# Half of the fourth batch's query projection moved from slot 1 to slot 0, a fifth gap in slot 0, and the first gate weights requested at the opening of slot 1

## The chip, the cores and the metric

The kernel runs on one core of a Trainium2 chip. The time is the device time of one execution in microseconds (us); the kernel before has a median of 847.64 us over 3 runs (847.49 to 848.31). The core has five engines: TensorE (PE, matmuls; its weight loads are shown as PEld), VectorE (DVE), ScalarE (ACT), GpSimd (POOL) and SyncE (SP, which here issues nearly all DMA transfers from one queue in order). Each engine works through its own list of instructions in order and waits on semaphores for the others.

## What is computed

One transformer block in float32 on `x` of 4 batches x 512 tokens x 512 features: attention after a layer norm, added to `x`, and then a gated feed-forward network after another layer norm, added again.

```python
def _layernorm(x, axis=-1, eps=1e-05):
    m = jnp.mean(x, axis=axis, keepdims=True)
    v = jnp.var(x, axis=axis, keepdims=True)
    return (x - m) / jnp.sqrt(v + eps)

# attention: 32 query heads, 8 key/value heads, 16 features per head
q = (resid @ Wq).reshape(B, T, N_HEADS, D_HEAD).transpose(0, 2, 1, 3)
k = (resid @ Wk).reshape(B, T, N_KV_HEADS, D_HEAD).transpose(0, 2, 1, 3)
v = (resid @ Wv).reshape(B, T, N_KV_HEADS, D_HEAD).transpose(0, 2, 1, 3)
q = q * cos + _rotate_half(q) * sin
k = k * cos + _rotate_half(k) * sin
att = einsum('bhgqd,bhkd->bhgqk', qg, k) / math.sqrt(D_HEAD)
att = jnp.where(causal, att, -jnp.inf)
ctx = einsum('bhgqk,bhkd->bhgqd', softmax(att), v)
out = ctx.reshape(B, T, D_MODEL) @ Wo

# feed-forward, hidden width 1376
y = (silu(xt @ W_gate.T) * (xt @ W_up.T)) @ W_down.T

x = x + attention(_layernorm(x))
x = x + feed_forward(_layernorm(x))
```

## The kernel before

Batches are counted from 0, so "the fourth batch" is batch 3. The program is one long list of instructions whose order is written out by hand. Its backbone is the attention of 32 **groups**; a group is one batch, one of four blocks of heads and one half (`GROUPS`), and there are eight to a batch. While a group's exponentials, masks and averages (`averages`, L1113, the matmuls named `av`) are made, the scores of the group two further on are taken for their bounds: each group has four **visits** (`visits`), in each of which `both_scores` (L1022, matmuls named `sc`) fills two pairs of PSUM banks, ScalarE takes exponentials of one (`exponentials`, tile `e`), and VectorE finds each row's bound in the other (`greatest`, L1035, tile `low`). A **last visit** (`last_visit`, L1056) follows and then the averages. The masks of `e` are made on POOL (`causal`, L1096). `masked` (L972) prepares a group's queries `qa` on POOL, and `turned_round` and `laid_out` carry the bounds to them through DRAM, one group ahead of their use.

**Slots.** `slot(b, steps)` (L1239) runs the eight groups of batch `b` and lays a list of **dense steps**, which belong to other work, into the gaps between the visits. Each step is a pair of a nominal cost in us and a closure. `gap(n)` adds `shares[n] / 8` of the list's total cost to the allowance, and `fill` (L1206) takes steps while the cost done, plus half the next step's, is within it. Slot 0 uses its first shares tuple and four gaps a group; slots 1 to 3 use the second tuple and a fifth gap, after the averages.

**Projections.** `projections(b, n)` (L375) gives, for a batch, `begin`, four steps `turned` and 48 steps `rest`: 8 for the keys, 8 for the first block of queries, 8 for the values and 8 for each of three further blocks of queries. A step of 0.43 nominal us (0.45 for values) is an eighth of a 512-column product; steps 0 to 3 of a key or query block use tokens 0 to 255, steps 4 to 7 tokens 256 to 511. A finished block of keys or queries is **rotated** (`rotated`, L347): two halves on VectorE (0.73 and 0.69) with a product or sum each on POOL. In slot 0 (`copied`) ScalarE first copies the bank to SBUF. Keys are also **spread** (`spread` in `keys`, L419): one shuffle on VectorE and four operations on POOL, at L425. The weights `wq`, `wk` and `wv` lie in the tile `shared` (`flat`), of which the gate and up weights later take three places in turn: place 2 is that of `wk` and `wv`, places 0 and 1 that of `wq`.

**Normalised rows.** For batches 2 and 3, `begin` puts twelve steps into the queue `calm`: statistics (kinds "a" and "b") and the normalisation (kind "c", L401) of each of four tiles of 128 tokens, on ScalarE, with three small POOL operations for each "b". One calm step is taken at each call of `odd_steps` (L259), except in visit 3, where `holding` is set. For batch 3 each "c" then puts a **flip** into the queue `aside`: `flipped` (L311) transposes the tile on VectorE in blocks (L314), writes it to DRAM with four DMAs (L318, `flip<-u`), and loads the tile before it back turned (L320, `xnT<-flip`, 256 KB); with the last tile both remaining loads go out. "Flip 1" and "load 1" are those of tile 1, and so on, from 0 to 3. `tail(i)` in `turned` takes from `calm` or `aside` until tile `i` is flipped, before the keys' first step.

**Helper queues.** `odd_steps(us, banks)` is called in every visit after `greatest` with a budget of us for VectorE: in slot 0 1.3, 0.95, 0.95 and 1.05 in visits 0 to 3, and 1.4 after the averages. With `banks` at 2 (visit 0) it takes waiting rotation halves (`full`) ahead of the queue `aside`, with 1 behind it, with 0 none. `holding` keeps POOL's work in visit 3 back until `last_visit` has issued `masked`.

**The seam.** `early` is the list of slot 0: what is left of batch 1's projections, batch 2's whole projections, and batch 3's keys, first query block and values. The copies of gate and up weights within DRAM (`copies`) are threaded into its first 40 steps. The list of slot 1 starts with `start1`: the twelve steps of batch 3's second query block and half its third, the output projection of batch 0 (`attended`, L492; its `outp` takes four products, one for each of `cx[0]` to `cx[3]`, per tile of 128 tokens, in two portions of 1.72), `load_f(0)`, the remaining twelve steps of queries with the tail of the second layer norm, and `load_f(1)`. `load_f` (L538) requests the gate and up weights of one block of 128 hidden features. Then follows the feed-forward network of batch 0 (`ordinary`, `edge`, `down`).

Of the kernel before, what the change touches and what calls it, by code (L numbers as in the profile page):

```python
# [74 lines left out]
def preln_block_kernel(  # L75
# [99 lines left out]
    def load_w(t, src):  # L175
        nc.sync.dma_start(out=t, in_=src.rearrange("(k p) m -> p k m", p=P))
# [3 lines left out]
    thin = [True]  # L180
# [4 lines left out]
    def emptied(n):  # L185
        for _ in range(n):
            for _, step in full.popleft():
                step()
# [70 lines left out]
    def odd_steps(us, banks=1):  # L259

        if calm and not holding[0]:
            calm.popleft()()
        for n in range(len(soon)):
            left, step = soon.popleft()
            if left > 0:
                soon.append((left - 1, step))
            else:
                aside.appendleft(step)
        while True:
            bank = full and full[0]  # L270
            queue = (unread and later) or (banks == 2 and bank) or aside or (banks and bank) or later
            if not queue:
                return
            us -= queue[0][0]
            if us < -0.15:
                return
            do(queue)
            if full and not full[0]:
                full.popleft()
# [4 lines left out]
    def pool_steps(n):  # L284
        for _ in range(min(n, len(idle))):
            idle.popleft()[1]()
# [251 lines left out]
    def load_f(f):  # L538
        if f < whole:
            wgu[f] = shared[:, (f + 2) % 3, :, :, :]  # L540
            for a, w in enumerate((wg, wu)):
                load_w(wgu[f][:, a, :, :], w[:, ts(f, P)])
# [76 lines left out]
    def after(step):  # L619
        return 0.0, step  # L620
# [401 lines left out]
    def both_scores(h, g, visit):  # L1022


        for c, i, j, heads in visit:
            for late in (False, True):
                for r in heads:
                    if h < len(GROUPS):
                        plain_half(h, r, i, plain[:, r % 2, c : c + P * (i + 1)], 0 if late else 64)
                    else:  # L1030
                        less_half(g, r, j, plain[:, r % 2, c : c + T - P * j], 64 if late else 0)
                for r in (2, 3) if heads[0] == 0 else (0, 1):
                    less_half(g, r, j, less[:, r % 2, c : c + T - P * j], 64 if late else 0)
# [16 lines left out]
    def all_greatest(h, visit):  # L1050
        if h < len(GROUPS):
            for c, i, j, heads in visit:
                for r in heads:
                    greatest(h, r, i, plain[:, r % 2, c : c + P * (i + 1)])

    def last_visit(h, g):  # L1056

        for r in range(4):
            less_score(g, r, 2, pairs[r // 2][:, r % 2, : 2 * P])
        if h < len(GROUPS):  # L1060
            for half in (64, 0):
                for r in range(4):
                    plain_half(h, r, 1, pairs[r // 2][:, r % 2, 2 * P :], half)
        for n in (0, 1):
            heads = slice(2 * n, 2 * n + 2)
            exponentials(e2[:, heads, :], pairs[n][:, :, : 2 * P])
            causal(e2, 0, heads)
        holding[0] = False
        masked(g + 3)
        release()  # L1070
        if h < len(GROUPS):
            for r in range(4):
                greatest(h, r, 1, pairs[r // 2][:, r % 2, 2 * P :])

    def turned_round(g):
        if g >= len(GROUPS):
            return
        t = small.tile([P, 32], F32, tag="turned", name="turned", bufs=2)
        nc.vector.transpose(t, low[g % 3])
        nc.sync.dma_start(out=lowest[g % 2], in_=t)  # L1080

    def laid_out(g):

        if g >= len(GROUPS):
            return
        rows = qa[g].rearrange("(r s) (i a q) -> r s i a q", r=4, i=NT, a=4)[:, 16 * (1 - GROUPS[g][2])]
        src = lowest[g % 2].rearrange("(a u r i) q -> u i r a q", a=4, u=2, r=4)[0]
        for a in (0, 2):
            nc.sync.dma_start(out=rows[:, 0, a : a + 2], in_=src[0][:, 2 - a : 4 - a])
        for i in range(1, NT):  # L1090
            nc.sync.dma_start(out=rows[:, i], in_=src[i])

    def exponentials(dst, src):
        nc.scalar.activation(dst, src, AF.Exp, scale=1.0 / math.sqrt(DH))  # L1094

    def causal(e, c, heads=slice(0, 4), exchanged=False):  # L1096

        for rows, base in ((slice(0, 64), -64), (slice(64, P), 0)) if exchanged else ((slice(0, P), 0),):
            nc.gpsimd.affine_select(  # L1099
                out=e[rows, heads, c : c + P],  # L1100
                in_=e[rows, heads, c : c + P],
                compare_op=ALU.is_ge,
                fill=0.0,
                base=base,
                pattern=[[0, heads.stop - heads.start], [1, P]],
                channel_multiplier=-1,
            )
# [65 lines left out]
    begin3, turned3, rest3, _ = projections(3, 3)  # L1173
    begin2, turned2, rest2, load2 = projections(2, 2)
    begin1, turned1, rest1, _ = projections(1, 1, then=load2)
# [30 lines left out]
    def fill(steps, upto, done):  # L1206
        while steps and done + steps[0][0] / 2 <= upto:
            cost, step = steps.popleft()
            step()
            done += cost  # L1210
            if not thin[0]:
                do(aside)
        return done
# [25 lines left out]
    def slot(b, steps):  # L1239

        steps = deque(steps)
        total = sum(cost for cost, _ in steps)
        done, part = 0.0, 0.0
        groups = range(8 * b, 8 * b + 8)
        thin[0] = copied[0] = b == 0
        narrow[0] = True

        shares = (0.2, 0.225, 0.2875, 0.2875, 0.0) if thin[0] else (0.19, 0.19, 0.22, 0.22, 0.18)

        def upcoming(n):  # L1250

            upto, us = part + total * shares[n] / 8, 0.0
            for cost, _ in steps:
                if done + us + cost / 2 > upto:
                    break
                us += cost
            return us

        def gap(n):
            nonlocal done, part  # L1260
            part += total * shares[n] / 8
            pool_steps((3, 2, 2, 0, 3)[n])
            done = fill(steps, part, done)

        for g in groups:
            h = g + 2
            laid_out(g + 1)
            for n, visit in enumerate(visits):
                e = (e0, e0, e1, e1)[n]
                if h < len(GROUPS):  # L1270
                    both_scores(h, g, visit)
                    exponentials(e[:, slice(0, 2) if n % 2 else slice(2, 4), :], less)
                elif n % 2 == 0:
                    both_scores(h, g, visit)
                    exponentials(e[:, 2:4, :], less)
                    exponentials(e[:, 0:2, :], plain)
                if n == 1:
                    causal(e0, 0)
                if n == 3:
                    causal(e1, 0)  # L1280
                    causal(e1, 3 * P, exchanged=True)
                all_greatest(h, visit)
                holding[0] = n == 3
                if thin[0]:
                    odd_steps((1.3, 0.95, 0.95, 1.05)[n], (2, 1, 1, 0)[n])
                else:
                    odd_steps(min(0.8 * upcoming(n) - (0.4, 0.4, 0.8, 0.8)[n], 2.3))
                gap(n)
            last_visit(h, g)
            turned_round(h)  # L1290
            averages(g)
            odd_steps(1.4)
            if not thin[0]:
                gap(4)
        thin[0] = copied[0] = narrow[0] = False
        emptied(len(full))
        if b == B - 1:
            do(later, len(later))
        for cost, step in steps:
            step()  # L1300
# [10 lines left out]
        nc.scalar.dma_start(out=homes[1], in_=spill)  # L1311

    turns = [step for pair in zip(turned2, *[iter(rest1[-8:])] * 2) for step in pair]
    early = [*rest1[16:-8], *turns, begin3, *rest2, *turned3, *rest3[:-24]]
    for u in range(whole):
        early.insert(4 * u + 4, after(lambda u=u: copies(u)))
    slot(0, early)
# [1 line left out]
    before, behind = attended(0, by_pe=(2, 3))  # L1319
# [18 lines left out]
    for u in range(whole):  # L1338
# [3 lines left out]
        asides += [(at + 1.0 * n, lambda n=n, combine=combine: combine(n)) for n in range(4)]  # L1342
    asides += [(6.0, spilled), (34.0, load_down), (34.1, load_rest)]
    start1 = [
        before[0],
        *rest3[-24:-12],
        *before[1:],
        after(lambda: load_f(0)),
        *rest3[-12:-1],
        *behind,  # L1350
        rest3[-1],
# [16 lines left out]
    before, behind = attended(1)  # L1368
# [15 lines left out]
    before, behind = attended(2)  # L1384
# [3 lines left out]
    before, behind = attended(3)  # L1388
# [36 lines left out]
```

## Time and profile before

| | |
|---|---|
| Median of 3 runs | 847.64 us (847.49 to 848.31) |
| The profiled execution | 848.06 us, of which the span 845.8 us |
| TensorE busy | 822.5 us, 97% of the span |
| VectorE, POOL, ScalarE busy | 545.5, 352.5 and 231.3 us |
| DMA traffic | 101.57 MB, mean 120 GB/s |
| Slot 0 (its first scores to those of slot 1) | 49.8 to 173.6 us |
| Granted TensorE clock | 1.00 |

A profile line of the timeline reads: start and length in us, engine, source line, operation, what it writes and reads, shape, and count; in brackets the engine's idle time just before, and what ended it. On TensorE matmuls are pipelined, and their modelled ends overlap the next start by some 0.07 us. A line of busy time by stretch reads: the stretch, its length, then busy us (and instructions) of PE, PEld, DVE, ACT and POOL, the granted clock, the DMA share and GB/s. The names in the profile are those of tiles, and several things share one tile: `wd_sb` also holds batch 3's projections and batch 1's turned rows; `xnT` stands for two tiles, one of which is batch 3's.

### The profile page before, as it was taken

To read this page: it belongs to the slowest core of one execution; us is meant where nothing else is said; L and a number is where in the kernel's file an instruction comes from. 1 tells how busy PE (TensorE), PEld (TensorE's weight loads), DVE (VectorE), ACT (ScalarE), POOL (GpSimd) and SP (SyncE) were. 2 spreads that over 40 slices of the span, in tenths; PEclk is the share of its full clock that TensorE was granted. 3 is DMA by queue.
4 is the path that set the end of the run, shared out by engine and by line. 5 is a ranking of instruction groups with operands and counts; after the bars stand their busy time and mean duration, and the time that the engine had idled before them with its cause. 6 is when DMAs were issued, how large, how long until landed. Compare 5 with 4: busy or idle time off the path is not lost.

```text
span 845.8 us, 28256 instructions
## 1 busy us (share of the span) xinstructions
PE 822.5 (97%) x11980; PEld 452.2 (53%) x11980; DVE 545.5 (65%) x1601; ACT 231.3 (27%) x342; POOL 352.5 (42%) x514
## 2 busy tenths in 40 slices
PE   6999999999999999999999999999999999999998
PEld 5654444544333335333555555436655556788887
DVE  7877777778555554458677776686877633656632
ACT  1045654422232322222233232222323331011100
POOL 4575574773544344223265634532244444101130
PEclk9999999999999999999999999999999999999999
DMA  8533304003764742253344632325333534545811
GB/s 259 124 96 78 91 16 91 5 3 64 232 191 144 235 137 77 88 200 77 84 155 140 196 115 66 115 47 151 96 97 103 162 106 148 119 146 174 291 33 50
DMA packets 149517, 101.57 MB, mean 120 GB/s; under 512 B 59696, under 2 KB 137264, under 8 KB 149136
## 3 DMA queue, kind: packets, MB, share of 16 engines
q1 hardware_dynamic: 149104, 94.01, 38.3%
q10 hardware_dynamic: 288, 5.77, 1.8%
q8 instruction: 94, 1.54, 0.8%
q14 instruction: 31, 0.25, 0.1%
HBM read 78.32 MB, written 25.17 MB: 122 GB/s over the span
## 4 chain that ended last, share of the span: by engine, by line
PE 76%; DVE 12%; POOL 4%; DMA 3%; issue 2%; ACT 1%; SPq 1%; POOLq 0%; DVEq 0%; ACTq 0%
PE mm L299 38%; PE mm L296 14%; PE sc L993 12%; DVE junk L1039 6%; PE av L1121 6%; PE sc L1006 4%; PE mm L590 2%; POOL e L1099 1%; DMA shared<-packed 1%; PE mm L582 1%; DVE st L218 1%; DVE rot L358 1%; ACT e L1094 1%; POOL home L425 1%; POOL qa L978 1%
## 5 line engine op out<-in xcount | busy, mean ns | idle before, releaser
L1039 DVE CUSTOM_DVE_ANT_0 junk<-sc,mask 128x128 f32<-128x128 f32 (+3 forms) x512 | 251.2, 491 | 139.0 <-PE sc L1006 78.4
L1094 ACT ACTIVATE e<-sc 128x1024 f32<-128x1024 f32 (+1 forms) x192 | 165.5, 882 | 384.4 <-PE sc L1006 300.7
L299 PE MATMUL mm<-xnT,shared 128*32 128x256 f32 (+1 forms) x3520 | 244.2, 420 | 2.3 <-DMA shared<-in_wg 1.5
L1099 POOL TENSOR_SCALAR_AFFINE_SELECT e<-e 128x512 f32<-128x512 f32 (+2 forms) x192 | 105.7, 560 | 225.4 <-ACT e L1094 222.3
L299 PEld LDWEIGHTS mm<-xnT,shared 128*32 128x32 f32 x3520 | 116.9, 110 | 113.0 <-issue 62.8
L993 PE MATMUL sc<-home,qa 32*64 32x512 f32 (+6 forms) x2048 | 156.1, 421 | 6.5 <-DVE low L1039 3.0
L1006 PE MATMUL sc<-qa,home 32*64 32x512 f32 (+6 forms) x2048 | 152.2, 427 | 1.5 <-DVE low L1039 0.8
L993 PEld LDWEIGHTS sc<-home,qa 32*64 32x64 f32 x2048 | 66.8, 131 | 90.2 <-DVE low L1039 29.1
L1121 PE MATMUL av<-e,home 128*32 128x512 f32 (+3 forms) x1024 | 81.9, 438 | 1.8 <-POOL e L1099 1.6
L296 PE MATMUL mm<-xnT,shared 128*128 128x256 f32 x360 | 80.3, 383 | 1.0 <-DMA shared<-packed 1.0
L296 PEld LDWEIGHTS mm<-xnT,shared 128*128 128x128 f32 x360 | 68.3, 192 | 12.8 <-issue 2.2
L299 PE MATMUL mm<-wd_sb,home 128*32 128x256 f32 (+3 forms) x848 | 71.4, 470 | 0.0
L1006 PEld LDWEIGHTS sc<-qa,home 32*64 32x64 f32 x2048 | 58.8, 130 | 22.5 <-issue 8.7
L1121 PEld LDWEIGHTS av<-e,home 128*32 128x32 f32 x1024 | 30.5, 109 | 47.2 <-issue 35.0
L299 PEld LDWEIGHTS mm<-wd_sb,home 128*32 128x32 f32 (+1 forms) x848 | 28.2, 110 | 36.9 <-issue 28.2
L299 PE MATMUL mm<-wo_sb,cx 128*32 128x512 f32 x384 | 45.4, 595 | 0.0
L797 POOL TENSOR_TENSOR wd_sb<-home 128x256 f32<-128x256 f32 x15 | 11.4, 759 | 75.6 <-DVE home L721 75.3
L1039 DVE DVE_READ_ACCUMULATOR2_ANT low<- 128x1 f32 x512 | 42.4, 83 | 0.0
L221 POOL TENSOR_TENSOR rstd<-rstd,neghalf 128x1 f32<-128x1 f32 x24 | 16.0, 667 | 56.8 <-DVE rstd L220 56.7
L1145 POOL TENSOR_TENSOR inv<-us,inverse 128x256 f32<-128x256 f32 x32 | 20.9, 654 | 44.5 <-DVE inverse L1138 44.3
L359 POOL TENSOR_TENSOR rot<-rot,rope_sb 128x512 f32<-128x512 f32 x18 | 25.7, 1425 | 23.0 <-DVE rot L358 22.8
L721 POOL TENSOR_TENSOR home<-home,u 128x512 f32<-128x512 f32 x20 | 25.2, 1281 | 21.2 <-DVE u L757 21.2
(146 smaller groups left out, 855.6 us busy)
## 6 DMA issues: line engine op xcount, KB each, us to landing
shared<-packed SPq DMA_DIRECT2D x90, 256.0 KB
flip<-u SPq DMA_DIRECT2D x88, 64.0 KB
packed<-xnT SPq DMA_DIRECT2D x10, 512.0 KB
xnT<-flip SPq DMA_DIRECT2D x18, 256.0 KB
wd_sb<-differences SPq DMA_DIRECT2D x7, 640.0 KB
shared<-packed SPq DMA_DIRECT2D x30, 128.0 KB
rows<-in_x SPq DMA_DIRECT2D x14, 256.0 KB
out<-rows SPq DMA_DIRECT2D x13, 256.0 KB
```

The costliest lines, as they stand in the source:

```text
L296: nc.tensor.matmul(out, lhsT=lhsT, rhs=rhs, start=start, stop=stop)
L299: nc.tensor.matmul(out[c : c + 32], lhsT=lhsT[:, c : c + 32], rhs=rhs, start=start, stop=stop)
L359: put(lambda: engine.tensor_tensor(rot, rot, sin, ALU.mult))
L590: nc.tensor.matmul(ps[96:P, ts(q, P)], lhsT=rest_w[:, a, kq, 32 * q : 32 * q + 32], rhs=xnTs[0][:, kq, most:], start=kq == 0, stop=kq == N ...
L721: engine.tensor_tensor(g, g, t, ALU.mult)
L993: nc.tensor.matmul(dst[at : at + 64, :n], lhsT=qa[g][rows_of(r), q : q + 64], rhs=keys_of(g)[rows_of(r), :n], start=True, stop=True,)
L1006: nc.tensor.matmul(dst[at : at + 64, first_q:], lhsT=keys_of(g)[rows_of(r), k : k + 64], rhs=qa[g][rows_of(r), P * j + first_q :], start=True,
L1039: nc.vector.tensor_tensor_reduce(out=junk[:, :n], in0=src, in1=mask[:, T - n : T] if i else mask[:, T:], scale=-1.0, scalar=BIG, op0=ALU.a ...
L1094: nc.scalar.activation(dst, src, AF.Exp, scale=1.0 / math.sqrt(DH))
L1099: nc.gpsimd.affine_select(out=e[rows, heads, c : c + P], in_=e[rows, heads, c : c + P], compare_op=ALU.is_ge, fill=0.0, base=base, pattern ...
L1121: nc.tensor.matmul(av[32 * r : 32 * r + 32, P * j :], lhsT=v[:, j, 4 * (m // 2) + r, DH * (1 - hf) : DH * (3 - hf)], rhs=e[:, r, c : c + n ...
L1145: nc.gpsimd.tensor_tensor(us[m][:, :, hf, :], turned[0][:, :, hf, :], by, ALU.mult)
```

## The change

Twelve of the 24 query steps of batch 3 that slot 1 ran first are put at the end of slot 0's list (one whole block of queries and half the next). Slot 0's nominal total goes from 47.00 to 52.16 us and slot 1's from 117.82 to 112.66. Slot 0 gets the fifth gap that the other slots have, with a share of 0.07, and the other four shares are scaled. `load_f(0)` is put ahead of batch 0's output projection as the first step of slot 1.

```diff
-        shares = (0.2, 0.225, 0.2875, 0.2875, 0.0) if thin[0] else (0.19, 0.19, 0.22, 0.22, 0.18)
+        shares = (0.19, 0.21, 0.265, 0.265, 0.07) if thin[0] else (0.19, 0.19, 0.22, 0.22, 0.18)
...
             averages(g)
             odd_steps(1.4)
-            if not thin[0]:
-                gap(4)
+            gap(4)
...
-    early = [*rest1[16:-8], *turns, begin3, *rest2, *turned3, *rest3[:-24]]
+    early = [*rest1[16:-8], *turns, begin3, *rest2, *turned3, *rest3[:-12]]
...
     start1 = [
-        before[0],
-        *rest3[-24:-12],
-        *before[1:],
         after(lambda: load_f(0)),
+        *before,
         *rest3[-12:-1],
```

`before[0]` is the opening of `attended(0)`, which does nothing for batch 0.

## The prediction

> **What bounds the kernel now.** I read the page's busy line first, then the busy time per group of heads, then TensorE's own timeline at the places that the change touches, and last SyncE's queue.
>
> ```profile
> PE 822.5 (97%) x11980; PEld 452.2 (53%) x11980; DVE 545.5 (65%) x1601; ACT 231.3 (27%) x342; POOL 352.5 (42%) x514
> ```
>
> TensorE is busy for 97%, so the sum is made on its order of work: what is moved costs nothing only where it fills a hole. The next view gives the busy time for two groups of slot 0 (the second is group 5) and one of slot 1.
>
> ```profile
> 111.40:128.01 16.61, 15.05 (x313) 7.50 (x313) 12.69 (x46) 8.57 (x14) 12.15 (x20) 1.00 0.13 21
> 128.01:143.15 15.14, 14.50 (x273) 6.77 (x273) 11.32 (x37) 8.23 (x12) 6.91 (x12) 1.00 0.48 90
> 222.23:243.80 21.57, 21.57 (x291) 7.44 (x289) 12.22 (x40) 6.39 (x8) 8.19 (x14) 1.00 0.78 256
> ```
>
> The reader is to see the first two numbers after the stretch, length and TensorE busy: slot 0 leaves 0.6 to 1.6 us of holes in a group, slot 1 none. A step taken out of slot 1 is worth its whole 0.43 us (seven steps ran in 3.23 us at 174.98, less some 0.2 of drain).
>
> **The fifth gap.** TensorE at the end of groups 5 (slot 0) and 9 (slot 1):
>
> ```profile
> 140.60 2.38 PE L1121 MATMUL av<-e,home 128*32 128x512 f32 x32
> 143.15 0.65 PE L993 MATMUL sc<-home,qa 32*64 32x512 f32 x2 [0.17 <-POOL qa L978]
> 143.98 0.60 PE L1006 MATMUL sc<-qa,home 32*64 32x512 f32 x2
> ...
> 216.43 2.44 PE L1121 MATMUL av<-e,home 128*32 128x512 f32 x32
> 218.60 3.70 PE L299 MATMUL mm<-xnT,shared 128*32 128x512 f32 x32
> 222.75 0.59 PE L1006 MATMUL sc<-qa,home 32*64 32x512 f32 x2
> ```
>
> In slot 0 the next scores wait for POOL's `masked` and then start staggered: from the end of the averages (142.98) to the end of the scores (144.58) is 1.60. With dense work between it is 223.34 - 218.87 = 4.47, less 3.44 of that work (two portions of 1.72) = 1.03. By the shares and the rule in `fill`, slot 0 gets 3, 3, 4, 4 and 1 steps in every group's gaps. One step then makes 1.46: 0.14 less than now, with a step more done. Eight groups: **-1.1** (at worst, if the wait stays, +3.4; at best -1.9, if the stagger's 0.33 goes beside it).
>
> **The four other steps.** The same rule leaves four visits of slot 0 one step short today (groups 0, 2, 4 visit 2, group 7 visit 0), as here:
>
> ```profile
> 90.59 1.50 PE L299 MATMUL mm<-xnT,shared 128*32 128x256 f32 x24
> 92.65 0.69 PE L1006 MATMUL sc<-qa,home 32*64 32x256 f32 x16 [0.56 <-DVE low L1039]
> ```
>
> Holes of 0.53 to 0.56, where a full visit keeps 0.13: one step of 0.43 fits, **0** (if the hole is not there, +1.7). VectorE's `greatest` is the cover and sets the visit's length either way. What the twelve moved steps issue beyond matmuls goes to group 7 (one ScalarE copy of 0.57, rotation halves of 0.73 and 0.69 on VectorE, 1.29 and 1.28 on POOL); there these engines are busy 6.4, 11.4 and 10.2 of 15.1 us now: 0.
>
> **Keys spread.** The second step of `keys`, four POOL operations (3.01 us at 121.44), comes ahead of the masks of `e` in group 4, and averages wait: 123.99 to 127.84 is 3.85 against 2.38. With the new order batch 2's spread falls into visit 3 of group 3, where `holding` puts it behind `masked`: the 1.42 goes. Behind it on POOL now stand the statistics of batch 3's second tile, for which ScalarE waits; I price that at 0.5 (POOL's 3.0 less the 2.5 that they have). **-0.9** (-1.4 to +0.5). Batch 3's own spread moves to group 7, where no statistics stand ahead of it: 0 (up to +1.4, the price in group 4).
>
> **What the earlier keys run into.** This decides. Dense work is now spread over 52.16 nominal us instead of 47.0, so batch 3's `turned3` and first key step come at 36.52/52.16 of slot 0, in visit 2 of group 5, not visit 1 of group 6. But the normalised rows come from `calm`, one step per call of `odd_steps`, and that clock doesn't move: the last falls into visit 2 of group 5 as before. SyncE's queue there:
>
> ```profile
> 132.16 1.94 SPq L318 DMA_DIRECT2D flip<-u  x4
> 134.14 0.51 SPq L320 DMA_DIRECT2D xnT<-flip  x1
> 134.75 2.20 SPq L318 DMA_DIRECT2D flip<-u  x4
> 137.06 1.92 SPq L320 DMA_DIRECT2D xnT<-flip  x1
> 139.02 2.22 SPq L318 DMA_DIRECT2D flip<-u  x4
> 141.35 3.33 SPq L320 DMA_DIRECT2D xnT<-flip  x2
> ```
>
> These are the flips and loads of tiles 1 to 3; the fourth load leaves at 144.30, traffic ends before 147.0, and the first key step runs at 147.16: no slack of note today. I count from the scores of visit 1 in group 5 (130.96 now).
>
> - Demand: visit 2's scores start at +2.68 and take 1.0, three query steps 1.29: the first key step at +5.0.
> - Supply: visit 0's budget of 1.3 now goes to batch 2's rotations (0.73 + 0.69), so flip 1 slips to visit 1, behind `greatest` (+2.62) and its transpose of 0.71: SyncE from +3.4. Then 1.94 and 0.51; flip 2 waits for VectorE until +6.4 and takes 2.20; load 1 leaves at +8.65, and its data are through 4.0 later (from 137.06 to 141.1 today, when the stretch has moved the 1,024 KB of two flips and two loads): +12.6. First wait 7.6.
> - Steps 0 to 3 need tokens 0 to 255 alone; after one step, visit 3's scores and three steps TensorE is at 12.6 + 0.43 + 1.0 + 1.29 = +15.4. Flip 3 leaves 1.96 after load 1, load 3 another 5.28 later (139.02 to 144.30) and is through in 2.4: +18.3. Second wait 2.9.
> - Step 4 ends at +18.7, where the last visit's scores begin; now they begin at +8.69 (139.65). Cost **+10.0**.
>
> Bounds: flip 3 can't leave VectorE before +6.4, so step 4 can't end before 6.4 + 5.28 + 2.4 + 0.43 = +14.5: 5.8 at least. If the first key step waits for all four loads, +18.3 + 0.43 + 1.0 + 1.72 = +21.5: 12.8. Load 0 left while flip 1 was still landing, so regions are told apart: I take 10.0. Behind load 3 on SyncE stand the next bounds (144.72), which are needed a group later. Nothing hides the wait: scores stand behind the key step in TensorE's queue, and VectorE, ScalarE and POOL wait for those.
>
> After such a wait the array may run slower at first. The kernel's opening is the nearest row:
>
> ```profile
> 6.03 1.12 PE L304 MATMUL mm<-ident,xa 128*128 128x128 f32 x4 [6.03 <-DVE xa L226]
> ...
> 75.81 0.66 PE L304 MATMUL mm<-ident,xa 128*128 128x128 f32 x4
> ```
>
> Sixteen transposes took 4.4 us against 2.64 warm, so up to 1.8 per wait, although the granted clock reads 1.00. After the first wait it falls into the second one's time; I take 0, and 1.8 as the end above. [...]
>
> **Slot 1.** Twelve steps fewer: 12 x 0.43 = **-5.16**. They covered something: the output projection needs the last group's `cx`.
>
> ```profile
> 178.31 0.69 DVE L1151 STREAM_TRANSPOSE cx<-inv 128x512 f32<-128x512 f32 x1
> 182.42 3.64 PE L299 MATMUL mm<-wo_sb,cx 128*32 128x512 f32 x32
> ```
>
> Averages ended at 173.54, `cx` at 179.0: 5.46 later. VectorE's queue there keeps its length (three rotation halves ahead of `greatest` replace two and the shuffle behind it). TensorE now reaches the fourth product of the first output tile 1.46 + 3 x 0.86 = 4.04 after the averages: **+1.4** (0 to 2.3).
>
> **The gate weights.**
>
> ```profile
> 213.63 1.92 PE L299 MATMUL mm<-xnT,shared 128*32 128x512 f32 x16 [1.46 <-DMA shared<-in_wg]
> ```
>
> `load_f(0)` stood behind flips in SyncE's queue until 208.71. Its place held batch 3's key and value weights, last read in group 7, so at the opening of slot 1 it leaves at once, behind group 9's small reads and ahead of nothing urgent: the turned bounds of the next group come a group later. **-1.46** (at least -0.5: VectorE's copy of the last tile ended at 213.1; a score burst now lies between).
>
> **Sum.** -1.1 + 0 - 0.9 + 10.0 - 5.16 + 1.4 - 1.46 = +2.8 us on the profiled execution's 848.06 (span 845.8 and 2.26 around it): 850.8. That execution was 0.42 above the median, so **850.4** beside 847.64.
>
> **Rivals.**
> - *The wait takes all four loads.* For it: all four go to one tile, and SyncE's queue is one. Against: the fourth load alone waited for the last flip. 12.8 for 10.0: 853.2, 855.0 with a slow array.
> - *The wait is short.* Flip 1 keeps visit 0 and loads issue in 0.51 as load 0 did: 5.8 for 10.0 gives 846.2.
> - *No wait at the keys* (the other side). Place: visit 2 of group 5. If the transposed rows lie there by +5.0, the rest counts alone: 850.4 - 10.0 = 840.4. It decides as soon as the wait is under 7.2 us. For it: TensorE never waited for batch 3's rows in the profile. Against: ScalarE's last normalisation ended at 136.60 (+5.6), after the demand.
> - *The weights bring nothing*, because the copy of the last tile ends as late: 851.4 at the bound of 0.5.
>
> **Chances.** Forecast with the weights' case 0.62, all four loads 0.12, short wait 0.11, no wait 0.15. A measurement of this kernel can't tell 0.2% (1.7 us) from no change. The short wait's 846.2 lies within that, with a tail on both sides: faster 0.15, same 0.08, slower 0.77. The range leaves out the case without a wait and little else: from the short wait with `cx` in time (844.8, cut to 845.5) to 855.0. The likeliest case alone: 848.5 to 852.5.
>
> **What would show it.** TensorE idle for some 7 us ahead of batch 3's first key step, released by a DMA `xnT<-flip`, and again some 3 us three steps later; `sc` after every `av` of slot 0 without the wait for `qa`; no 0.5 us holes in groups 2, 4, 7; the averages of group 4 at 2.4; a hole of 1.4 ahead of the first `wo_sb,cx`; none for `in_wg`. The prediction is wrong if the keys start without a hole, or if the flips leave VectorE a visit earlier than I have them.

## The result, and the profile after

The changed kernel takes 857.39 us (median of 6 runs, 854.32 to 858.23), the kernel before 847.85 us (6 runs): a ratio of 1.0105, 95% interval 1.0088 to 1.0121. It is 9.5 us slower. The profiled execution took 857.04 us with a span of 855.2 us.

The page's busy line, after:

```profile
PE 826.0 (97%) x11980; PEld 454.8 (53%) x11980; DVE 546.7 (64%) x1601; ACT 232.2 (27%) x343; POOL 354.2 (41%) x514
```

The work is the same but for one ScalarE copy. TensorE's busy time grew by 3.5 us with the same 11,980 matmuls, so some of them took longer, and it stood still for 5.9 us more (855.2 - 826.0 against 845.8 - 822.5).

TensorE's waits from 60 to 240 us, after (what waited and for whom: us in total, times, longest):

```profile
PE mm L299 <- DMA xnT<-flip: 6.4, 1, 6.4
PE mm L304 <- ACT xa L401: 3.9, 2, 1.9
PE mm L299 <- DVE cx L1151: 2.1, 1, 2.1
```

The same list before had none of the three. The first is the wait at batch 3's keys, and the third the one for `cx`; the second is at batch 2's transposes, which the prediction does not mention.

Busy time for six groups of slot 0 and the first of slot 1, after (stretch and length; busy us of PE, PEld, DVE, ACT, POOL; granted clock, DMA share, GB/s):

```profile
66.02:81.31 15.29, 15.07 (x274) 7.37 (x272) 9.91 (x37) 10.12 (x18) 8.45 (x14) 1.00 0.51 132
81.31:103.52 22.21, 18.10 (x275) 8.43 (x273) 11.67 (x41) 9.74 (x15) 9.87 (x14) 0.85 0.25 68
103.52:118.72 15.20, 14.77 (x348) 8.69 (x345) 12.02 (x41) 8.69 (x17) 10.17 (x15) 1.00 0.02 5
118.72:133.97 15.25, 14.73 (x283) 7.15 (x281) 11.55 (x41) 9.16 (x15) 12.14 (x20) 1.00 0.13 22
133.97:157.47 23.50, 16.81 (x282) 7.67 (x281) 12.26 (x41) 8.24 (x12) 8.66 (x13) 0.85 0.39 81
157.47:172.63 15.16, 14.64 (x324) 8.00 (x320) 12.20 (x42) 6.26 (x8) 10.17 (x12) 1.00 0.03 6
187.78:213.72 25.94, 23.86 (x299) 7.91 (x297) 20.30 (x59) 5.20 (x6) 11.68 (x15) 0.93 0.16 34
```

Groups 1, 3 and 6 are as long as before, though each does one step more. Group 2 has gone from 15.21 to 22.21, group 5 from 15.14 to 23.50, group 4 from 16.61 to 15.25. The granted clock, third number from the end of a line, is under 1.00 just where a wait lies.

The starts of the averages place the whole difference. At group 7's averages the changed kernel is 13.9 us behind, at group 8's 17.8, at group 9's 14.1, at group 15's 10.3, and it ends 9.4 behind. Slot 0 lost 13.9 us, the opening of slot 1 lost 3.9, and the rest of slot 1 won 7.4 back; some 0.9 more came later, most of it a wait of 0.99 us for weights near the end that is absent here.

### The profile page after: what moved, and what is told of

Its sections match the earlier page's. It is cut to its first block, busy times and chain, and to the rows that moved or that the text cites. A ratio compares the mean times of both kernels' runs of the same rounds, so it can differ in the third digit from the quotient of the medians.

```text
span 855.2 us, 28256 instructions
## 1 busy us (share of the span) xinstructions
PE 826.0 (97%) x11980; PEld 454.8 (53%) x11980; DVE 546.7 (64%) x1601; ACT 232.2 (27%) x343; POOL 354.2 (41%) x514
## 4 chain that ended last, share of the span: by engine, by line
PE 82%; DVE 11%; DMA 2%; issue 2%; POOL 1%; ACT 1%; SPq 0%; DVEq 0%; POOLq 0%; ACTq 0%
PE mm L299 38%; PE mm L296 17%; PE sc L993 13%; PE av L1121 8%; DVE junk L1039 7%; PE sc L1006 4%; PE mm L590 2%; PE mm L582 1%; PE mm L304 1%; DVE rot L358 1%; DVE st L218 1%; ACT e L1094 1%; POOL e L1099 0%; DMA flip<-u 0%; DVE u L314 0%
## 5 line engine op out<-in xcount | busy, mean ns | idle before, releaser
L299 PE MATMUL mm<-xnT,shared 128*32 128x256 f32 (+1 forms) x3520 | 246.9, 421 | 7.0 <-DMA xnT<-flip 6.4
L1006 PE MATMUL sc<-qa,home 32*64 32x512 f32 (+6 forms) x2048 | 154.8, 432 | 1.3 <-DVE low L1039 0.6
```

The costliest lines, as they stand in the source:

```text
L299: nc.tensor.matmul(out[c : c + 32], lhsT=lhsT[:, c : c + 32], rhs=rhs, start=start, stop=stop)
L1006: nc.tensor.matmul(dst[at : at + 64, first_q:], lhsT=keys_of(g)[rows_of(r), k : k + 64], rhs=qa[g][rows_of(r), P * j + first_q :], start=True,
```

## The experiments

Edits are given against the changed kernel unless another is named. All compare with the kernel before, timed on the same chip in the same session; its medians there lie between 847.65 and 847.74 us, so that the medians may also be set beside the changed kernel's 857.39. What is said of groups and waits is read from one profiled execution of each kernel.

### Batch 2's transposes put back

```diff
-    turns = [step for pair in zip(turned2, *[iter(rest1[-8:])] * 2) for step in pair]
-    early = [*rest1[16:-8], *turns, begin3, *rest2, *turned3, *rest3[:-12]]
+    last1 = rest1[-8:]
+    turns = [turned2[0], *last1[:2], turned2[1], *last1[2:7], turned2[2], last1[7]]
+    rest2 = [*rest2[:4], turned2[3], begin3, *rest2[4:]]
+    early = [*rest1[16:-8], *turns, *rest2, *turned3, *rest3[:-12]]
```

> The changed kernel with batch 2's third and fourth transposes put back to the visits that they had before (visits 1 and 2 of group 2; the request for batch 3's rows goes behind the fourth one). Theory (the transposes came one visit too early for ScalarE's normalisation, and each wait slows the array for some us after it): the two waits of 1.93 us and the slow matmuls behind them go, group 2 falls from 22.2 to 15.2 us, the time from 857.4 to 850.4. Rival (group 2's loss is DMA traffic, 236 to 321 GB/s in that stretch from the request for batch 3's rows): the slow matmuls stay and move with the request, some 3 us are left, 853.5.

Measured: 850.13 us, ratio 1.0028 (1.0016 to 1.0040). From group 2's averages to those of group 4, the profile stands within 0.1 us of the kernel before, where the changed kernel was 7.17 behind at group 2. Both waits and the slow matmuls are gone (four transposes take 0.66 us at 84.95 and again at 89.01), although the request for batch 3's rows is still made there: the theory holds, and the rival falls.

ScalarE's timeline of the changed kernel shows the wait's cause:

```profile
82.70 1.03 ACT L1094 ACTIVATE e<-sc 128x1024 f32<-128x1024 f32 x1 [2.21 <-PE sc L1006]
83.62 0.80 ACT L401 ACTIVATE xa<-xa,mean,rstd 128x512 f32<-128x512 f32 x1
```

and TensorE's there (dense work alone, score rows left out):

```profile
84.47 1.07 PE L304 MATMUL mm<-ident,xa 128*128 128x128 f32 x4 [1.93 <-ACT xa L401]
85.47 1.94 PE L299 MATMUL mm<-wd_sb,shared 128*32 128x256 f32 x16
90.66 0.66 PE L304 MATMUL mm<-ident,xa 128*128 128x128 f32 x4 [1.94 <-ACT xa L401]
```

In each visit ScalarE first takes the exponentials of the scores that have just ended, then one calm step. The third tile's transposes are now the first dense step of the very visit that holds its normalisation, so TensorE waits for an exponential and a normalisation, 1.03 + 0.80 with the handover. In the kernel before they came one visit later. Its ScalarE normalised the third tile in the visit ahead of the one in which TensorE turned it, and TensorE found it ready:

```profile
83.44 0.80 ACT L401 ACTIVATE xa<-xa,mean,rstd 128x512 f32<-128x512 f32 x1
84.95 0.66 PE L304 MATMUL mm<-ident,xa 128*128 128x128 f32 x4
```

### Batch 3's normalisation at twice the pace

```diff
             calm.popleft()()
+            if calm and brisk[0]:
+                calm.popleft()()
...
             if b > 1:
+                brisk[0] = b == 3
```

> The changed kernel with batch 3's normalisation taken two steps per call instead of one, so that its flips go out some five visits earlier; the keys stay where the change put them. Theory (the keys wait for the loads of batch 3's turned rows): the 6.4 us wait ahead of the first key step and the slow matmuls behind it go, group 5 falls from 23.5 to 15.2 us, the time from 857.4 to 849.1. Rival (the wait is that of SyncE's queue or of DMA bandwidth and moves along with the flips; or ScalarE, now with two steps a visit, makes the scores wait): less than half of the 8.3 comes back, 853 to 857.

Measured: 850.45 us (847.01 to 853.68 over ten runs), ratio 1.0030 (1.0017 to 1.0043). From the averages of group 4 to those of group 5 the profile now loses 0.3 us against the kernel before, where the changed kernel lost 6.9. It still waits 1.76 us there, ahead of the fifth key step, which needs the last two tiles; the 1.4 us that averages no longer lose in group 4 make up for it. The theory holds for the wait, and the rival falls. The profiled execution is the fastest of the ten; the last section sets the spread of their times beside their granted clocks.

### Cover for `cx`

```diff
         after(lambda: load_f(0)),
+        *rest3[-12:-8],
         *before,
-        *rest3[-12:-1],
+        *rest3[-8:-1],
```

> The changed kernel with four of batch 3's query steps put ahead of batch 0's output projection at the opening of slot 1. Theory (the output projection waits for the last group's cx, which the moved steps used to cover): 1.72 of the 2.08 us wait are covered and the slow matmuls behind it (about 1.9 us) go too; 857.4 falls by 3.2 to 4.0, to about 853.8. Rival (the loss at the opening of slot 1 is VectorE's longer queue there, the rotations of two query blocks): the wait moves to the next scores, 856 to 857.4.

Measured: 855.32 us (853.75 to 857.63 over four runs), ratio 1.0091 (1.0075 to 1.0108). That is 2 us less than the changed kernel and not 3.2, and with four runs so far apart the two intervals overlap: by the times alone the gain is not shown, and what follows is read from the profile. The wait for `cx` is gone from the profile. By the starts of the averages, 3.9 us lost from group 7 to 8 became 1.0, but group 9 then won back 2.2 instead of 3.6: seven query steps instead of eleven now stand between the output projection and the feed-forward network, and TensorE waits 0.5 us there for the load of that network's rows (`xnT<-flip`). Cover taken from one wait opened another.

### All three together

> All three edits in one kernel. Theory (the three waits are separate and add up): 7.0 + 8.3 + 3.6 off 857.4, 838.5, which is 9 us below the kernel before. Rival (part of what one wait costs is hidden by another, or TensorE meets another wait as soon as these go): 842 to 848.

Measured: 844.89 us (842.21 to 850.10), ratio 0.9977 (0.9958 to 0.9995). The rival: TensorE meets other waits. The profile shows 2.02 us ahead of batch 3's fifth key step, since the last flip still left VectorE only in visit 1 of group 5, and 0.89 ahead of the first gate product.

### TensorE kept at work while it waits

`fill_in` is 11 for tiles 2 and 3 of batch 2; the second part runs ahead of batch 3's first key step.

```diff
         pt = bank()
+        for _ in range(fill_in):
+            nc.tensor.transpose(pt[:, :P], ident, ident)
...
+                    ps = bank()
+                    for _ in range(13):
+                        product_of(ps[:, : 2 * P], wk_sb[:, 0, :], xnTs[0][:, 0, : 2 * P], True, True)
```

> The changed kernel with TensorE kept at work in its waits: eleven extra 128x128 transposes of the identity ahead of each of batch 2's third and fourth tiles (about 1.8 us of the 1.93), and thirteen extra key products of 0.43 us ahead of batch 3's first key step (5.6 of the 6.42), all into banks that are overwritten or not read. The waits stay as long as they are. Theory (the array's clock falls because TensorE stood still): the granted clock stays at 1.00 there, the slow matmuls in groups 2 and 5 (about 3.1 and 2.2 us) go, 857.4 falls to about 852. Rival (the slow matmuls come from something else in these stretches, such as the loads of 190 to 320 GB/s): they stay slow, 857 or more.

Measured: 855.05 us (853.27 to 857.00 over four runs), ratio 1.0088 (1.0073 to 1.0104), 2.3 us under the changed kernel and not 5. The intervals of the two overlap, so the reading rests on the profile. First two stretches of the changed kernel (columns as above), then the same two of this one:

```profile
84.00:86.00 2.00, 1.52 (x12) 0.97 (x16) 1.36 (x4) 0.84 (x2) 1.25 (x1) 0.64 0.02 2
86.00:88.00 2.00, 2.00 (x24) 0.63 (x24) 0.00 (x0) 0.17 (x1) 1.80 (x2) 0.51 0.23 35
```

```profile
84.00:86.00 2.00, 1.43 (x17) 0.85 (x18) 1.85 (x5) 1.25 (x3) 0.77 (x1) 1.00 0.01 1
86.00:88.00 2.00, 2.00 (x32) 0.78 (x25) 0.27 (x1) 0.45 (x2) 1.92 (x2) 1.00 0.11 17
```

The granted clock stays at 1.00. From the averages of group 1 to those of group 2 this kernel loses 3.9 us, the two waits alone, where the changed kernel lost 7.0: the other 3.1 was the slow array. The rival falls: the slow stretches moved 2 and 35 GB/s. At the opening of slot 1, where nothing was added, the clock stays at 1.00 as well; the wait of 2.1 us is still there, and the loss goes from 3.9 to 2.7. In group 5 nothing comes back (7.8 us lost instead of 6.9). TensorE's own rows show one reason:

```profile
146.76 0.64 PE L299 MATMUL mm<-xnT,shared 128*32 128x256 f32 x8 [1.91 <-DMA xnT<-flip]
148.27 1.50 PE L299 MATMUL mm<-xnT,shared 128*32 128x256 f32 x24
151.35 0.64 PE L299 MATMUL mm<-xnT,shared 128*32 128x256 f32 x8 [1.58 <-DMA xnT<-flip]
```

With the array at full speed the steps in between end sooner, and the fifth key step waits for the last two tiles. The other reason is the first wait, which did not stay as long as it was: the four writes of flip 2 held SyncE's queue for 3.00 us and not 2.02, and the first key step came 1.1 us later in its group; why is open. In the changed kernel the traffic of the last loads ended at about 152.1 us. By an estimate from its first key step (148.32) and the 3.0 us that the four steps and the scores ahead of the fifth take at full speed (146.76 to 149.77 above), a second wait of some 0.8 to 1 us would have stood there, and the slow matmuls, which cost 1.9 (5.45 us from the first key step to the last visit's scores, against 3.6 at full speed), covered that much.

### The fifth gap alone

The edit is against the kernel before.

```diff
-        shares = (0.2, 0.225, 0.2875, 0.2875, 0.0) if thin[0] else (0.19, 0.19, 0.22, 0.22, 0.18)
+        shares = (0.19, 0.21, 0.265, 0.265, 0.07) if thin[0] else (0.19, 0.19, 0.22, 0.22, 0.18)
...
-            if not thin[0]:
-                gap(4)
+            gap(4)
```

> The kernel before with the fifth gap and its shares alone; no step is moved between the slots, so one step a group goes from the visits to the place behind the averages. Theory (a step there is free, since the scores behind it wait for POOL's masked anyway, and VectorE sets the length of the visits): 0 to -1.1 us, 846.6 to 847.7. Rival (the step costs its 0.43 there and the visits don't get shorter): +3.4, 851.

Measured: 848.41 us beside 847.69, ratio 1.0008 (0.9998 to 1.0018). Clearly not +3.4, so a step there does not cost its 0.43; but no gain shows either. In the profile seven groups are within 0.2 us of their length before, and group 5 is 1.35 longer: its last scores wait 1.47 us for VectorE, which itself waited 1.91 us for the writes of flip 2. The gap is worth something only when there are more steps to put in.

### The early request alone

The edit is against the kernel before.

```diff
 start1 = [
+        after(lambda: load_f(0)),
         before[0],
         *rest3[-24:-12],
         *before[1:],
-        after(lambda: load_f(0)),
```

> The kernel before with load_f(0) at the opening of slot 1 alone. Theory (the first gate product waits for a request that stood behind the flips in SyncE's queue): -1.46 us, 846.3, with no wait ahead of that product. Rival (the wait passes to the copy of the last turned tile): -0.5 or less, 847.2.

Measured: 848.08 us beside 847.69, ratio 1.0003 (0.9995 to 1.0012). The rival was right. TensorE at the first gate product of this kernel:

```profile
213.62 0.64 PE L299 MATMUL mm<-xnT,shared 128*32 128x256 f32 x8
215.31 1.92 PE L299 MATMUL mm<-xnT,shared 128*32 128x512 f32 x16 [1.05 <-DVE xnT L307]
```

Of the 1.46 us, 1.05 pass to VectorE's copy of the last turned tile. In the changed kernel's order a burst of scores falls between the transposes and that product, and TensorE goes on without a wait.

### Eight steps moved instead of twelve

Batch 2's transposes are put back and the pace is doubled here too.

```diff
-    early = [*rest1[16:-8], *turns, *rest2, *turned3, *rest3[:-12]]
+    early = [*rest1[16:-8], *turns, *rest2, *turned3, *rest3[:-16]]
...
+        *rest3[-16:-8],
         *before,
-        *rest3[-12:-1],
+        *rest3[-8:-1],
```

> The changed kernel with batch 2's transposes put back and batch 3's normalisation two steps per call, and with eight instead of twelve query steps moved to slot 0; all eight of the next block stand ahead of batch 0's output projection. Against the kernel with all three edits, whose profile still shows 2.02 us ahead of batch 3's fifth key step and 0.6 us of small waits at the opening of slot 1, four steps go back (+1.7) and the keys come some 3.5 us later. Theory (what is left there is the late loads of batch 3's third and fourth tiles): no wait at the keys, -2.0 and -1.0 against +1.7: about 1 us under it, 843.5. Rival (the keys' wait moves with them): 845 to 847.

Measured: 848.29 us (845.75 to 851.07), ratio 1.0005 (0.9993 to 1.0017). A miss. The keys no longer wait. But the eight steps push the output projection back and leave seven behind it, and the feed-forward network stands still for its rows; the sixteen products behind this wait take 2.75 us, where sixteen such took 1.92 in the profile of the early request:

```profile
212.20 2.75 PE L302 MATMUL mm<-xnT,shared 128*32 128x512 f32 x16 [2.71 <-DMA xnT<-flip]
```

### Two flips more in group 4

The edit is against the kernel with all three edits; the second kernel leaves out the cover for `cx`.

```diff
     rest2 = [*rest2[:4], turned2[3], begin3, *rest2[4:]]
+    for at in (32, 29):
+        rest2.insert(at, after(lambda: do(aside)))
```

> The kernel with all three edits, and two more flips of batch 3 taken in visits 1 and 2 of group 4, so that the last flip leaves VectorE there and not in visit 1 of group 5. Theory (the 2.02 us that its profile still shows ahead of batch 3's fifth key step are the load of the last tile): that wait goes, 844.9 falls to 842.9. Rival (two more transposes in these visits make the scores wait as long, or the array's slow phases set the spread anyway): 844 to 846.

> The same without the four query steps ahead of the output projection, so the wait for cx at the opening of slot 1 stays (2.08 us, and up to 1.9 of slow matmuls) and the small waits that those four steps brought (0.6, 0.35 and 0.89 us in the profile) go. Theory: 2.08 + 0 to 1.9 less 1.8, 843 to 845. Rival (the four steps are worth their whole 3.9): 846.8.

Measured: 842.04 us, ratio 0.9933 (0.9911 to 0.9956), with the cover for `cx`; 841.17 us (840.32 to 842.06), ratio 0.9918 (0.9899 to 0.9936), without. The wait at the keys is gone in both, as in the theory. The second has the lowest median of the study (its interval overlaps with the first's), 6.5 us under the kernel before and 16 under the changed one: every step stands where the change put it but for two transposes, and the normalisation, the flips and the request for batch 3's rows are set to the new pace. Both are below what was expected for them. TensorE's waits from 60 to 240 us in the second (its lines are numbered three or four higher):

```profile
PE sc L1010 <- DVE low L1043: 1.8, 2, 1.4
PE sc L997 <- DVE low L1043: 1.7, 6, 0.6
PE mm L302 <- DVE cx L1155: 0.7, 1, 0.7
```

The wait of 1.4 us is new: it stands at the last scores of group 4, behind the flips that were put there. The `cx` wait is 0.7 us and not 2.1, and VectorE's rows show why: here two rotation halves (0.75 and 0.69) stand ahead of `greatest` and `cx`, where the changed kernel had three (0.63, 0.75 and 1.55).

## Why the prediction was right and wrong

The sign, and the place and kind of the wait at the keys, were right. The size was not: +2.8 us was forecast and +9.5 measured, outside the range.

- **What was left out: batch 2's transposes.** The step that failed is the first under "What the earlier keys run into". It says that all dense work of slot 0 comes earlier while `calm` keeps its clock, and then draws the consequence for batch 3 alone. Batch 2's rows come from the same queue. Its third and fourth transposes stood one visit behind their normalisation before, and the same arithmetic of shares moves them into the same visit. The sum thus has them at nothing; they measured 7.0 us, shown by putting just these back (-7.3 us in the median, group 2 as before). With them put back the kernel takes 850.13 us, where 850.4 was forecast for the change. That it fits so closely is luck in part: the terms below were off by 0.5 to 2.5 us each, in both directions, and nearly cancel.
- **The slow array** was priced at 0, on the ground that it falls into the second wait. In group 5 that ground held in part: of the 1.9 us that the slow matmuls cost, the second wait would have taken some 0.8 to 1 (an estimate, above). Group 2 and the opening of slot 1 have no second wait, and 3.1 us in two waits and 1.2 us in one were lost there, inside the numbers above and below (1.2 is 3.9 less the 2.7 of the two profiles whose clock stayed up, with a mean of 1.00, those of the doubled pace and of TensorE kept at work). The stated end of 1.8 per wait was about the right size. Behind the waits of 1.93 and 1.94 us in group 2 the granted clock read 0.50 to 0.51 (the last section has what the traces show of it).
- **The wait at the keys**: 10.0 forecast; group 5 grew by 8.4. Flip 1 slipped to visit 1 as worked out. The first wait was 6.42 and not 7.6, mainly because load 1 was through 3.14 us after it left SyncE and not 4.0. It issued in 0.44 us and not 1.92, which may be the reason. The second wait, 2.9 by forecast, does not show in the changed kernel, and was 1.58 where the array stayed fast.

```profile
145.18 0.44 SPq L320 DMA_DIRECT2D xnT<-flip  x1
148.32 1.08 PE L299 MATMUL mm<-xnT,shared 128*32 128x256 f32 x8 [6.42 <-DMA xnT<-flip]
```

- **The output projection**: 1.4 forecast; the wait was 2.08, and with the slow matmuls slot 1's first group lost 3.9 (2.7 with the clock up). VectorE's queue did not keep its length: one of the three rotation halves there took 1.55 us where its like takes 0.69.
- **The fifth gap and the four short visits**: -1.1 and 0. Groups 1, 3, 6 and 7 came out at 0.00, -0.05, -0.16 and +0.02 (group 0 at +0.24), so the steps were free, as said, but the 0.14 a group did not come: in groups 0 to 4 the scores behind the gap still start staggered (1.24 us against 1.11).
- **Keys spread**: -0.9 forecast, group 4 fell by 1.36. (3.85 less 2.38 is 1.47; the prediction's sum has 1.42.) ScalarE's wait for the later statistics, priced at 0.5, did not show.
- **Slot 1 and the gate weights**: -6.6 forecast, -7.4 measured after its first group. No wait is left at the first gate product in the new order; the early request alone brought nothing measurable.

The rival without a wait at the keys was priced at 840.4. The kernel in which the waits are taken away, with the twelve steps in slot 0, measures 841.17: the gain was there. That the number agrees is luck in part. At group 7's averages its profile is 0.5 us behind the kernel before, where -2.0 was forecast (there is a new wait of 1.4 us in group 4, and the 1.1 of the fifth gap did not come), while slot 1 behind its first group won 7.5 and not 6.6, and another 1.0 came behind it, which was not forecast.

## What to carry to other kernels

When a list of work is paced by shares, adding to its end moves everything in it forward; go through each item that has a producer outside the list, not only the one nearest to the edit. Work handed out one piece per visit is a clock of its own, and has to be set anew with the list. And count what a wait of TensorE does to the matmuls behind it: here that was up to nearly as much again (3.1 us behind 3.9 us of waits).

## What the runs showed of the hardware

- **The clock falls after short waits, but not always.** In the changed kernel's profile both waits in group 2 (1.93 and 1.94 us) were followed by a granted clock of 0.50. With the doubled pace the same two waits (1.93 and 1.91) were there, and its profile reads:

```profile
84.67 0.66 PE L307 MATMUL mm<-ident,xa 128*128 128x128 f32 x4 [1.93 <-ACT xa L404]
89.29 0.66 PE L307 MATMUL mm<-ident,xa 128*128 128x128 f32 x4 [1.91 <-ACT xa L404]
```

```profile
88.00:90.00 2.00, 0.71 (x8) 0.55 (x12) 1.47 (x5) 1.25 (x3) 0.73 (x2) 1.00 0.95 227
90.00:92.00 2.00, 2.00 (x52) 1.09 (x52) 0.01 (x1) 1.15 (x2) 0.00 (x0) 1.00 0.96 340
```

  Four transposes take 0.66 us and the clock stays at 1.00, with 227 GB/s of transfers beside them and 340 behind, while the slow stretches of the changed kernel moved 2 and 35 GB/s: so it is not the traffic.
- **The length of a wait does not decide alone.** In the changed kernel's profile, read in stretches of 0.2 us, the granted clock is 0.50 from 84.6 to 88.0 us, from 91.4 to 94.8, from 146.0 to 152.8 and from 193.8 to 197.2. Each begins inside a wait or within 0.8 us of its end; the waits are 1.93, 1.94, 6.42 and 2.08 us long. With TensorE kept at work the wait for `cx` was 2.08 us long as well, and the eight products behind it took 1.07 us and not 1.91; the mean granted clock of that whole execution is 1.00. What else decides is not shown: no run moved a wait on purpose to test it.
- **The spread of the times goes with the clock**: the ten runs with the doubled pace lie between 847.01 and 853.68 us, with mean granted clocks from 1.00 to 0.992, and the six of the version with the lowest median, whose profile shows neither wait in group 2, between 840.32 and 842.06, with clocks of 0.999 and 1.00. Of the changed kernel's six runs the one at 854.32 us has a mean granted clock of 0.994, the others (857.04 to 858.23) 0.990.
- **A slow array can hide a wait**: keeping it busy brought 3.1 us in group 2 and nothing in group 5, where the next load became the limit (1.58 us) and the first one came later.
